# Merged depthwise kernels: stored with eight channels innermost, turned by TensorE, their zeros stored later

## The chip, the cores and the metric

One core of a Trainium2 chip runs the whole program. The metric is the time of one execution on the device in microseconds, the median over runs. Engine names: PE (TensorE: matmuls, with PEld its weight loads), DVE (VectorE), ACT (ScalarE), POOL (GpSimd), SP (SyncE, which here only issues DMAs). ACT, POOL and SP issue DMAs, each on a queue of its own; all queues share 16 DMA engines.

## The reference

Four layers on x of [8, 384, 32, 32], float32. Layer 0 is an RMS norm, a Mamba block run forwards and backwards over the 1024 pixels, and a gated 3x3 depthwise convolution. Layer 1 is a 1x1 / 3x3 / 1x1 convolution, linear attention and an MLP. The change touches what prepares layers 2 and 3, which are depthwise convolutions with large kernels:

```
# layer 2: seven depthwise convolutions (13x13, 5x5, 7x7, 7x7 dilated 2, 3x3 dilated 3, 4, 5), each
# with a batch norm, added up
out = bn_eval(dwconv(x, w_lk, 1), bn_gamma[0], ...)
for i, (w, r) in enumerate(zip(branch_ws, dilates)):
    out = out + bn_eval(dwconv(x, w, r), bn_gamma[i + 1], ...)
# layer 3: 1x1 product with a batch norm and a shortcut, then 13x13 depthwise + a scale per channel, GELU
x_pw = bn(einsum('bchw,oc->bohw', x, pw_w), ...) + x
out = bn(dwconv(x_pw, dwk_w), ...) + bn(x_pw * dw1_w, ...)
return gelu(out)
```

All kernels of a layer and their norms fold into one 13x13 kernel per channel (layer 2: `g2`, layer 3: `g3`) and one bias.

## The kernel before

**Stages.** A prologue (the first part of layer 0 for image 0, constants, and the merged kernels g2 and g3) leads into eight scans, one per image. Beside the scan of one image run the front of the next and layer 1 of the one before. After the last scan come the rest of layer 1 for the last image, convolution a (layer 2), the 1x1 product of layer 3 (`product`, `finish`) and convolution b (layer 3's 13x13).

**The prologue's chain.** `front(0)` loads x (`xi`), squares it on ACT, sums on PE (`ms_s`, `ms_b`), scales on DVE (`xn`), multiplies on PE (`in`), copies on ACT to `uz` and stores that to DRAM (`u_d`). From there it is loaded shifted (`ut`), convolved on PE (`c`), and passed through Silu on ACT (`uc`, L805). `dl_d` and `v_d` are then stored through POOL's queue and loaded by SP for the scan. In the scan, each unit is exponentials on ACT (`da`), products and scans on DVE (`du` L958, `hs` L970), a multiplication on POOL (L979) and sums on PE (`acc`).

**The merged kernels.** `kernels` (L171) runs interleaved with `front(0)`. For each third of the channels it loads the weights through SP, clears a tile of [128 channels, 4 shifts, 63 rows, 4 columns] on POOL (L205, L221), and merges the kernels into rows 25 to 37 of it with small DVE instructions (`merge`, L190, L192). The other rows stay zero: they are the border that makes a Toeplitz matrix of the row index. Six POOL DMAs of 504 KB (L216, L230) store the whole tiles, zeros included, to `g2_d` and `g3_d` in DRAM, channel outermost. The tiles are taken from the eight buffers `hs` that the scan uses later.

**The windows.** Convolutions a and b work on 48 blocks of eight channels. A block's weights are one tile `tp` of [128, 8, 128]: for each of four column shifts e, 32 partitions, one for each image row, hold the rows of the Toeplitz matrix. Each shift is one DMA of 128 KB (`load_windows`, L250). In DRAM, partition p starts 16 bytes after partition p-1, and each of the eight channels is a run of 512 bytes. There are 20 such tiles. For convolution a the first 20 blocks are loaded by POOL, from the moment when the scan's memory is free; the others, and those of convolution b, by SP and ACT in turn. In `conv` (L371) a group of four channels is four times four matmuls, which run side by side on four column groups of PE; their weights are the slice

```
tp[:, c, :].rearrange("p (j t) -> p j t", t=KT)[:, :, t]
```

that is, 32 elements at a step of 16 bytes. The images are loaded as `xt_a` (POOL, with a short SP load of the last image from `x2i_d`) and `xt_b` (POOL, from `xp_d`), and DVE copies them shifted. Results of a go through `yt` to `y2_d`, those of b through GELU on ACT (`ot`) to `out`, in pieces of 128 bytes.

**The order of the work.** The functions give only dependencies. The order on every engine is written by a planner (`Plan`): it places all instructions by rank (the longest way to the end, plus a number from the table `BIAS` for each family such as ('Pool', 'tp_a<g2_d')) with its own estimate of each one's duration. So a change in one place can move instructions anywhere. A DMA that is issued also waits for an earlier one whose completion counter it takes over; there are eight counters for POOL's DMAs and eight for those of SP and ACT.

Of the kernel before, what the change touches and what calls it, by code (L numbers as in the profile page):

```python
# [11 lines left out]
FP = mybir.dt.float32  # L12
# [61 lines left out]
def tile_layers(  # L74
# [44 lines left out]
    g2_d = dram.tile([C, NSH, TG, KT], FP, tag="g2_d", name="g2_d")  # L119
    g3_d = dram.tile([C, NSH, TG, KT], FP, tag="g3_d", name="g3_d")  # L120
# [50 lines left out]
    def kernels(small, large):  # L171
# [3 lines left out]
        off = H - 1 - KS // 2  # L175

        def merge(g, src, k, d, scale, first):
            lo = KS // 2 - d * (k // 2)

            step = NSH // gcd(NSH, d)  # L180
            for a in range(min(step, k)):
                n = len(range(a, k, step))
                kx = lo + d * a
                dst = g[
                    :, kx % NSH, off + lo : off + lo + d * (k - 1) + 1 : d,
                    kx // NSH : kx // NSH + (n - 1) * (d * step // NSH) + 1 : d * step // NSH,
                ].rearrange("p b a -> p a b")
                sv = src[:, a::step, :]
                if first:
                    nc.vector.tensor_scalar_mul(dst, sv, scale)  # L190
                else:
                    nc.vector.scalar_tensor_tensor(dst, sv, scale, dst, ALU.mult, ALU.add)  # L192

        def column(t, n, name):
            return t[:, :n].rearrange("p (q i t) -> p q i t", q=NSH, i=TG)
# [3 lines left out]
        gn = NSH * TG * KT  # L199
        for c in range(NC):  # L200
# [15 lines left out]
            nc.gpsimd.dma_start(g2_d[c * P : (c + 1) * P].rearrange("p q i t -> p (q i t)"), t[:, :gn])  # L216
# [9 lines left out]
            mid = g[:, m % NSH, off + m, m // NSH : m // NSH + 1]  # L226
# [3 lines left out]
            nc.gpsimd.dma_start(g3_d[c * P : (c + 1) * P].rearrange("p q i t -> p (q i t)"), t[:, :gn])  # L230
# [4 lines left out]
        yield 1  # L235

    wins = {}

    def load_windows(g_d, tag, n, queues, behind=None):
# [3 lines left out]
        tp = wins["pool"].tile([P, NCH, TP], FP, tag="tp", name=f"tp_{tag}_{n}", bufs=N_WIN)  # L243
        for e in range(NSH):
            at = H * ((n % 2 * 2 + e) % NSH)
            win = bass.AP(
                g_d.tensor, g_d[NCH * n, e, 0, 0].offset,
                [[KT, H], [NSH * TG * KT, NCH], [1, TP]],
            )
            made = queues[e % len(queues)].dma_start(tp[at : at + H], win)  # L250
# [5 lines left out]
    def windows(queues):  # L256
        for n in range(N_WIN):
# [5 lines left out]
              cw1_t, cw2_t, qkv_t, proj_t, w1, w2, headmask, mask8, mask8_t, kernels, windows)  # L263
# [5 lines left out]
    with tc.tile_pool(name="cx", bufs=2, reuse_waits="tile") as cxp, tc.tile_pool(  # L269
# [15 lines left out]
        def conv(g_d, src_d, last_d, tag, put, far):  # L285
# [67 lines left out]
            for g in range(NQ):  # L353
# [7 lines left out]
                for t in range(KT):  # L361
                    for e in range(4):
# [4 lines left out]
                        else:  # L367
# [5 lines left out]
                            tp[:, c, :].rearrange("p (j t) -> p j t", t=KT)[:, :, t], rhs,  # L373
# [116 lines left out]
def _layers01(tc, nc, B, xv, x2_d, x2i_d, dram, ident, mean_w, eps5, eps6, one, half, minus1, vec, bns, bnt,  # L490
              rs, rsm, inproj_t, xproj_t, dtproj_t, outproj_t, taps1, taps3, taps3b, sel, alog,
              cw1_t, cw2_t, qkv_t, proj_t, w1, w2, headmask, mask8, mask8_t, kernels, windows):
# [10 lines left out]
    with ExitStack() as ctx:  # L503
# [499 lines left out]
        def fold():  # L1003
# [37 lines left out]

        prepare = kernels(
            lambda name: scanp.tile([P, L], FP, tag="hs", name=name, bufs=N_HS),
            lambda name: scanp.tile([P, L], FP, tag="hs", name=name, bufs=N_HS),
        )
# [310 lines left out]
        jobs = [[first, 36, 0, rounds // 4, 0], [fold(), 36, 0, rounds, 0]]  # L1356
# [63 lines left out]
class Step:  # L1420
    def __init__(self, ins, kind_of):
# [28 lines left out]
        else:  # L1450
# [3 lines left out]
            if self.engine == "Pool":  # L1454
                self.ns = 80 + n * (2.21 if self.kind == "InstTensorTensor" else 2.55)
# [395 lines left out]
def draft(nc, tc, bias):  # L1851
# [15 lines left out]
BIAS = {('Activation', 'acc<y0'): -13900,  # L1867
 ('Activation', 'bc_d<xd'): -60800,
 ('Activation', 'center<center'): -86000,
 ('Activation', 'da<dlt'): 1600,  # L1870
 ('Activation', 'dl<dt'): -21300,
 ('Activation', 'dw<dw'): -18000,
 ('Activation', 'fold<fold'): -148900,
 ('Activation', 'gbias<biasq_d'): -35300,
 ('Activation', 'h_d<hh'): 31500,
 ('Activation', 'hh<h'): 600,
 ('Activation', 'hm<mf'): -501200,
 ('Activation', 'kp<phi_k'): -30300,
 ('Activation', 'kv<kvs'): -61000,
 ('Activation', 'kvp<kvp'): 315700,  # L1880
 ('Activation', 'kvp_d<kvp'): -900,
 ('Activation', 'lc<lc'): -7500,
 ('Activation', 'ms_r<ms_r'): -70000,
 ('Activation', 'ms_r<ms_s'): -2100,
 ('Activation', 'ot<cv_b'): -58600,
 ('Activation', 'out<ot'): 4700,
 ('Activation', 'phi_k<kv_kp'): 53000,
 ('Activation', 'phi_q<q'): -391200,
 ('Activation', 'qp<phi_q'): -2200,
 ('Activation', 'rz<den'): -3500,  # L1890
 ('Activation', 'rz<rz'): -7300,
 ('Activation', 'sq<xi'): -91600,
 ('Activation', 'tm<pw'): 145400,
 ('Activation', 'tp_b<g3_d'): -31500,
 ('Activation', 'u_d<uz'): -31400,
 ('Activation', 'uc<c1'): -11000,
 ('Activation', 'ud_d<ud'): -33900,
 ('Activation', 'uz<in'): 500,
 ('Activation', 'var_r<var_r'): 110900,
 ('Activation', 'var_r<var_s'): -14600,  # L1900
 ('Activation', 'vs<xx'): -111800,
 ('Activation', 'vt<kv_vt'): 2000,
 ('Activation', 'vt<ones'): 20900,
 ('Activation', 'x2_d<turn'): 53700,
 ('Activation', 'xd<xd'): 6900,
 ('Activation', 'xt_b<xp_d'): -50500,
 ('Activation', 'yf_d<yt'): 10800,
 ('Activation', 'yt<cv_a'): -38000,
 ('Activation', 'z_d<uz'): 140600,
 ('DVE', 'bias1<fold'): -72900,  # L1910
 ('DVE', 'bias2<bias2'): 191000,
 ('DVE', 'bias2<bn_t'): 26600,
 ('DVE', 'bias3<bn_t'): -43000,
 ('DVE', 'biasc<fold'): -4000,
 ('DVE', 'biasf<fold'): -122000,
 ('DVE', 'carry<hs'): 67300,
 ('DVE', 'dlt<pk'): 40000,
 ('DVE', 'du<vr'): -602900,
 ('DVE', 'dwh<pk'): -99500,
 ('DVE', 'g2<kw'): 15500,  # L1920
 ('DVE', 'g3<g3'): 28000,
 ('DVE', 'g3<k3'): 143300,
 ('DVE', 'hs<da'): 151900,
 ('DVE', 'kv<kvs'): 2000,
 ('DVE', 'lc<lc'): -96000,
 ('DVE', 'ln<xx'): -42300,
 ('DVE', 'qp<qp'): 59300,
 ('DVE', 'uc<dl'): -44000,
 ('DVE', 'ud<uc'): -36600,
 ('DVE', 'v2<pk'): -51500,  # L1930
 ('DVE', 'var_r<var_r'): -111500,
 ('DVE', 'var_r<var_s'): -214500,
 ('DVE', 'xn<xi'): 56200,
 ('DVE', 'xo0<tm'): 7000,
 ('DVE', 'xo1<tm'): 32500,
 ('DVE', 'xo2<tm'): -19000,
 ('DVE', 'xr<lc'): -35800,
 ('DVE', 'xt_a<xt_a'): 4200,
 ('DVE', 'xt_b<xt_b'): 3000,
 ('DVE', 'xx<c2'): 2300,  # L1940
 ('DVE', 'xx<op'): 46000,
 ('DVE', 'xx<pj'): 62500,
 ('DVE', 'zr<acc'): 16300,
 ('PE', 'acc<hs'): 1600,
 ('PE', 'acc<y0'): -4600,
 ('PE', 'c1<ut'): -35800,
 ('PE', 'c2<dw'): 21200,
 ('PE', 'center<fold'): 44100,
 ('PE', 'cv_a<xt_a'): -7500,
 ('PE', 'cv_b<xt_b'): -146300,  # L1950
 ('PE', 'den<qp'): 111100,
 ('PE', 'dt<xd'): -98100,
 ('PE', 'fold<bn_t'): 200,
 ('PE', 'fold<v2'): 13800,
 ('PE', 'h<xx'): 18800,
 ('PE', 'kss<spread'): -102400,
 ('PE', 'kvp<pj'): -65300,
 ('PE', 'kvs<zero'): -16000,
 ('PE', 'lc<lc_i0'): -81500,
 ('PE', 'mf<ln'): -4300,  # L1960
 ('PE', 'mo<hm'): 3100,
 ('PE', 'ms_b<ms_r'): -26700,
 ('PE', 'ms_s<sq'): -45000,
 ('PE', 'op<g'): 14200,
 ('PE', 'op<zr'): 20200,
 ('PE', 'pb<bias2'): 2500,
 ('PE', 'pj<qp'): 800,
 ('PE', 'pw<yp'): -12000,
 ('PE', 'q<xx'): 5300,
 ('PE', 'rzb<rz'): -12000,  # L1970
 ('PE', 'var_b<var_r'): -5500,
 ('PE', 'var_s<vs'): -37200,
 ('PE', 'var_s<xx'): -37300,
 ('PE', 'xd<uc'): -111000,
 ('Pool', 'dl_d<dl'): 19000,
 ('Pool', 'fold<fold'): 89500,
 ('Pool', 'g2<'): -4200,
 ('Pool', 'g2_d<g2'): -43500,
 ('Pool', 'g3<'): -5700,
 ('Pool', 'g3_d<g3'): -20000,  # L1980
 ('Pool', 'g_d<zr'): -18700,
 ('Pool', 'h_d<zero'): -78000,
 ('Pool', 'hs<hs'): -7300,
 ('Pool', 'spread<'): -10800,
 ('Pool', 'tp_a<g2_d'): -39000,
 ('Pool', 'turn<'): 51500,
 ('Pool', 'u_d<zero'): 17400,
 ('Pool', 'v_d<uc'): 229400,
 ('Pool', 'w1_d<fold'): 80300,
 ('Pool', 'x1_d<xr'): -300,  # L1990
 ('Pool', 'x2i_d<xx'): 148700,
 ('Pool', 'xn_d<xn'): -36200,
 ('Pool', 'xn_d<zero'): -18000,
 ('Pool', 'xp_d<xo0'): -23200,
 ('Pool', 'xp_d<xo1'): 60200,
 ('Pool', 'xp_d<xo2'): -48000,
 ('Pool', 'xt_a<'): -200,
 ('Pool', 'xt_b<xp_d'): 51700,
 ('Pool', 'y2_d<yt'): -36000,
 ('SP', 'bct<bc_d'): -7000,  # L2000
 ('SP', 'c1<c1_d'): -2000,
 ('SP', 'c2<c2_d'): -2000,
 ('SP', 'dlt<dl_d'): 19600,
 ('SP', 'dw_i0<h_d'): 2000,
 ('SP', 'dw_i1<h_d'): -23200,
 ('SP', 'dw_i2<h_d'): -10600,
 ('SP', 'dw_i3<h_d'): -202400,
 ('SP', 'g<g_d'): -5000,
 ('SP', 'k3<in_dwk'): 55000,
 ('SP', 'kvw<kvp_d'): -17800,  # L2010
 ('SP', 'kw<in_l2k'): 18200,
 ('SP', 'lc_i0<xn_d'): 610500,
 ('SP', 'lc_i1<xn_d'): 2000,
 ('SP', 'lc_i2<xn_d'): 12200,
 ('SP', 'lc_i3<xn_d'): 4000,
 ('SP', 'pj<in_proj_t'): -36600,
 ('SP', 't3<in_taps3'): 8000,
 ('SP', 't3b<in_taps3b'): 80000,
 ('SP', 'tp_a<g2_d'): 14500,
 ('SP', 'tp_b<g3_d'): 165900,  # L2020
 ('SP', 'turn<x2i_d'): 213400,
 ('SP', 'ut<u_d'): -183800,
 ('SP', 'w1<w1_d'): 125000,
 ('SP', 'w2<in_w2'): 4700,
 ('SP', 'win<in_inproj_t'): -42500,
# [124 lines left out]
```

## Time and profile before

| | |
|---|---|
| median of 3 runs | 4487.36 us (4484.69 to 4489.67) |
| the profiled execution | 4489.67 us, of which the profile's span is 4487.8 |
| PE, DVE, ACT, POOL busy | 3960.7, 3643.9, 2618.5, 2615.8 us |
| DMA | 748530 packets, 976 MB, 217 GB/s over the span |
| loads of windows (`tp_a`, `tp_b`) | 384 of 128 KB: 80 by POOL, 152 by SP, 152 by ACT |
| median time to landing | tp_a 8.1 (POOL), 7.3 (SP), 6.3 (ACT); tp_b 6.8 (SP), 6.1 (ACT) |
| stores of merged kernels | 6 of 504 KB, 9.5 us to landing |
| weight loads of convolutions a and b | 3072 each, 137 ns median |

Busy times overlap: what counts is which engine is full in which stage, and which wait ends last there. A line of the stages names begin and end in us, length, busy time of each engine with the number of instructions, the clock granted to PE, the share of time in which the 16 DMA engines were busy, and GB/s. A line of the chain names start, length and what the path to the end went through. A line of a DMA queue names packets, MB, and the time that its packets took as a share of 16 engines over the window; q0 is POOL's, q1 SP's and q10 ACT's queue. One MB is counted as a million bytes there, and KB of a load as 1024.

### The profile page before, as it was taken

The page shows a single profiled execution, that of the slowest core. Times are in us where ns is not written, and L with a number is a line of the kernel's source. Part 1 is how long each engine was busy: PE and PEld are TensorE (multiplying, and loading weights), DVE is VectorE, ACT ScalarE, POOL GpSimd, SP SyncE. Part 2 cuts the span into 40 slices and gives each one's busy share as a digit, 9 for nine tenths or more (in the row PEclk, how much of TensorE's full clock was granted, in tenths as well). Part 3 has the DMA queues.
Part 4 walks back from the last instruction along what each step waited for, and adds up shares of the span by engine and source line. Part 5 has one row for each costly group of instructions (what it writes and reads, how often), then busy time and mean ns, then how long its engine had stood idle before and what let it go on. Part 6 is the DMA issues. An engine that isn't in the chain of part 4 may idle for free.

```text
span 4487.8 us, 95449 instructions
## 1 busy us (share of the span) xinstructions
PE 3960.7 (88%) x38454; PEld 1600.2 (36%) x38454; DVE 3643.9 (81%) x3843; ACT 2618.5 (58%) x3701; POOL 2615.8 (58%) x1567
## 2 busy tenths in 40 slices
PE   5687798999988999999999899989889979989978
PEld 1121233233323332343333323332243433376456
DVE  2999989999999889999999899989999801176365
ACT  3666657865786578667866886578566503101212
POOL 2686757676667657775777576757675830043111
PEclk8687899999999999999999999999999969999989
DMA  9587786588658866896788668856845661398998
GB/s 263 187 256 254 244 233 232 201 256 252 225 197 252 251 224 206 258 269 207 239 248 256 208 225 252 261 200 229 232 136 171 194 151 51 88 242 220 270 200 160
DMA packets 748530, 976.06 MB, mean 217 GB/s; under 512 B 256840, under 2 KB 433464, under 8 KB 746552
## 3 DMA queue, kind: packets, MB, share of 16 engines
q1 hardware_dynamic: 504864, 680.88, 51.4%
q0 software_dynamic: 47616, 170.88, 11.7%
q10 hardware_dynamic: 195608, 118.21, 9.9%
q8 instruction: 303, 4.96, 0.5%
q14 instruction: 139, 1.14, 0.1%
HBM read 737.32 MB, written 232.40 MB: 216 GB/s over the span
## 4 chain that ended last, share of the span: by engine, by line
PE 49%; DVE 18%; DMA 15%; issue 7%; ACT 6%; POOL 2%; SPq 1%; ACTq 1%; DVEq 0%; POOLq 0%
DVE hs L970 11%; PE mo L623 8%; PE mf L623 7%; DVE du L958 4%; DMA dw_i<-h_d 3%; PE cv_a L371 3%; PE acc L643 3%; PE pj L623 3%; PE cv_b L371 2%; ACT da L953 2%; PE in L623 2%; PE q L623 2%; PE op L623 2%; PE kv_vt L623 2%; PE c L623 2%
## 5 line engine op out<-in xcount | busy, mean ns | idle before, releaser
L979 POOL TENSOR_TENSOR hs<-hs,bct 128x1024 f32<-128x1024 f32 x768 | 2174.3, 2831 | 884.4 <-DVE carry L975 498.9
L953 ACT ACTIVATE da<-dlt,neg_a 128x512 f32<-128x512 f32 x1536 | 1021.4, 714 | 577.8 <-DVE hs L970 461.0
L958 DVE TENSOR_TENSOR du<-vr,bct 128x1024 f32<-128x1024 f32 x768 | 979.9, 1276 | 54.3 <-DMA vr<-v_d 28.6
L970 DVE TENSOR_TENSOR_SCAN hs<-da,carry,du 128x512 f32<-128x512 f32 x768 | 946.4, 1267 | 39.4 <-PE acc L648 4.3
L970 DVE TENSOR_TENSOR_SCAN hs<-da,du 128x512 f32<-128x512 f32 x768 | 900.0, 1208 | 35.5 <-ACT da L953 9.0
L648 PE MATMUL acc<-hs,selt 128*32 128x512 f32 x2304 | 543.4, 634 | 78.9 <-POOL hs L979 78.6
L623 PE MATMUL mf<-ln,w 128*32 128x512 f32 x4608 | 579.1, 614 | 36.6 <-ACT uc L805 20.4
L623 PE MATMUL mo<-hm,w 128*32 128x512 f32 x4608 | 564.1, 595 | 0.3 <-DVE xx L1286 0.3
L643 PE MATMUL acc<-hs,selt 128*32 128x512 f32 x768 | 413.3, 627 | 22.6 <-POOL hs L979 22.5
L623 PE MATMUL in<-xn,win 128*32 128x512 f32 x2304 | 307.6, 629 | 24.7 <-DMA win<-in_inproj_t 15.4
L623 PEld LDWEIGHTS mf<-ln,w 128*32 128x32 f32 x4608 | 167.1, 113 | 383.9 <-issue 299.2
L953 ACT ACT_TABLE_LOAD x224 | 287.4, 1283 | 21.4 <-DMA dlt<-dl_d 7.5
L623 PEld LDWEIGHTS mo<-hm,w 128*32 128x32 f32 x4608 | 166.9, 110 | 325.3 <-issue 293.9
L648 PE MATMUL dw<-dw_i,t3b 96*32 96x512 f32 x1056 | 222.0, 686 | 16.2 <-DMA dw_i<-h_d 16.1
L371 PE MATMUL cv_b<-xt_b,tp_b 128*32 128x256 f32 x3072 | 192.6, 410 | 47.3 <-ACT ot L480 37.9
L313 POOL DMA_DIRECT2D xt_a<-x_d x48 | 40.1, 835 | 303.8 <-PE var_b L623 121.4
L344 DVE COPY xt_b<-xt_b 32x2496 f32<-32x2496 f32 x94 | 136.4, 1452 | 88.0 <-DMA xt_b<-xp_d 78.9
L371 PE MATMUL cv_a<-xt_a,tp_a 128*32 128x256 f32 x3072 | 179.1, 391 | 27.1 <-DVE xt_a L338 10.9
L648 PEld LDWEIGHTS acc<-hs,selt 128*32 128x32 f32 x2304 | 121.7, 114 | 173.7 <-POOL hs L979 144.2
L371 PEld LDWEIGHTS cv_b<-xt_b,tp_b 128*32 128x32 f32 x3072 | 147.3, 143 | 92.9 <-ACT ot L480 45.3
L371 PEld LDWEIGHTS cv_a<-xt_a,tp_a 128*32 128x32 f32 x3072 | 156.6, 139 | 50.0 <-issue 27.7
L623 PEld LDWEIGHTS in<-xn,win 128*32 128x32 f32 x2304 | 99.8, 115 | 196.4 <-issue 156.4
(211 smaller groups left out, 5637.9 us busy)
## 6 DMA issues: line engine op xcount, KB each, us to landing
dlt<-dl_d SPq DMA_DIRECT2D x384, 256.0 KB, 4.5
vr<-v_d SPq DMA_DIRECT2D x384, 256.0 KB, 5.0
bct<-bc_d SPq DMA_DIRECT2D x256, 256.0 KB, 5.3
ut<-u_d SPq DMA_DIRECT2D x192, 257.5 KB, 5.4
lc_i<-xn_d SPq DMA_DIRECT2D x192, 228.8 KB, 6.5
dw_i<-h_d SPq DMA_DIRECT2D x192, 228.8 KB, 6.2
w<-w_d SPq DMA_DIRECT2D x64, 576.0 KB, 6.6
w<-in_w SPq DMA_DIRECT2D x64, 576.0 KB, 5.3
```

Source lines behind the costliest of these rows:

```text
L313: nc.gpsimd.dma_start(own[:, 0:near], src_d[n].rearrange("h b c w -> h (b c w)"))
L344: nc.vector.tensor_copy(xt[at[e] : at[e] + e * H, :, 0 : RL - e - (e - 1)], xt[at[0] : at[0] + e * H, :, e : RL - (e - 1)],)
L371: nc.tensor.matmul(ps[H * e : H * (e + 1), 0:BW], tp[:, c, :].rearrange("p (j t) -> p j t", t=KT)[:, :, t], rhs, start=(t == 0), stop=(t = ...
L623: product = nc.tensor.matmul(ps[lo:hi], lhs[:, lo:hi], rhs, start=start, stop=stop, skip_group_check=True)
L643: first = product()
L648: tc.keep_in_program_order(product())
L953: nc.scalar.activation(da[:, bass.ts(j, HALF)], dlt[:, bass.ts(j, HALF)], AF.Exp, scale=neg_a[:, g, r : r + 1],)
L958: nc.vector.tensor_mul(pairs(du), pairs(vt), bct[r][:, 0:1, :].to_broadcast([P, 2, HALF]),)
L970: nc.vector.tensor_tensor_scan(t[:, s][:, way], da[:, s][:, way], du[:, s][:, way], k_c if second else 0.0, ALU.mult, ALU.add,)
L979: made.append(nc.gpsimd.tensor_mul(pairs(t), pairs(t), bct[r][:, 1:2, :].to_broadcast([P, 2, HALF])))
```

## The change

The merged kernels get another layout in DRAM: [48 blocks, 4 shifts, 63 rows, 4 columns, 8 channels], channels innermost. A row of a block is then 128 bytes, and the window of one partition is one run of 4 KB that starts 128 bytes after that of the partition before. The tile `tp` has the same order, so a matmul's 32 weights lie 128 bytes apart.

The tile in which DVE merges has 32 rows for each shift instead of 63, of which 13 are used. `turn` brings the channels innermost: 16 matmuls with the identity for each of the six tiles, and one ACT copy from PSUM to a tile `s2`, which permutes. `store` writes the 13 rows with kernel values, by four POOL DMAs for each tile (26.6 KB each, in pieces of 128 bytes). The zero rows are written from the tile `zero` by `borders`, eight POOL DMAs of 307 KB in pieces of 800 bytes, as a job within the first scan. The planner counts 100 ns more for a copy on POOL, and the table `BIAS` is replaced.

```diff
-    g2_d = dram.tile([C, NSH, TG, KT], FP, tag="g2_d", name="g2_d")
+    g2_d = dram.tile([NB_C, NSH, TG, KT, NCH], FP, tag="g2_d", name="g2_d")
...
-            return t[:, :n].rearrange("p (q i t) -> p q i t", q=NSH, i=TG)
+            return t[:, :n].rearrange("p (q i t) -> p q i t", q=NSH, i=H)
+
+        def store(g_d, g, c):
+
+            n = P // NCH
+            made = turn(g, f"{g_d.tensor.name}_{c}")
+            for q in range(NSH):
+                nc.gpsimd.dma_start(
+                    g_d[n * c : n * (c + 1), q, low : low + KS].rearrange("n i t c -> i n (t c)"),
+                    made[H * q : H * q + KS].rearrange("p (n w) -> p n w", n=n),
+                )
...
-        gn = NSH * TG * KT
+        gn = NSH * H * KT
...
-            nc.gpsimd.dma_start(g2_d[c * P : (c + 1) * P].rearrange("p q i t -> p (q i t)"), t[:, :gn])
+            store(g2_d, g, c)
...
+    def borders(zero, held):
+
+        info = mybir.DependencyInfo(mybir.DependencyClass.NoSync, mybir.DependencyReason.DATA)
+        low = H - 1 - KS // 2
+        half = NB_C * NSH // 2
+        part = low * KT * NCH // 4
+        src = zero[:half, 0:part]
+        src = bass.AP(src.tensor, src.offset, [src.ap[0], [0, 4], [1, part]])
+        for g_d in (g2_d, g3_d):
+            flat = g_d.rearrange("n e i t c -> (n e) (i t c)")
+            for p in range(2):
+                for at in (0, low + KS):
+                    dst = flat[p * half : (p + 1) * half, at * KT * NCH : (at + low) * KT * NCH]
+                    made = nc.gpsimd.dma_start(dst.rearrange("p (a b) -> p a b", a=4), src)
+                    tc.add_manual_dep(made.ins, held[0].ins.name, info, reason="later")
+                    yield 1
...
-        tp = wins["pool"].tile([P, NCH, TP], FP, tag="tp", name=f"tp_{tag}_{n}", bufs=N_WIN)
+        tp = wins["pool"].tile([P, H, KT, NCH], FP, tag="tp", name=f"tp_{tag}_{n}", bufs=N_WIN)
...
-                g_d.tensor, g_d[NCH * n, e, 0, 0].offset,
-                [[KT, H], [NSH * TG * KT, NCH], [1, TP]],
+                g_d.tensor, g_d[n, e, 0, 0, 0].offset,
+                [[NCH * KT, H], [1, NCH * TP]],
...
-                            tp[:, c, :].rearrange("p (j t) -> p j t", t=KT)[:, :, t], rhs,
+                            tp[:, :, t, c], rhs,
...
+        def turn(g, name):
+
+            ps = long_psum(f"kt_{name}")
+            t = s2(f"kt_{name}")
+            for a in range(KT):
+                for q in range(NSH):
+                    nc.tensor.matmul(
+                        ps[H * q : H * (q + 1), a * P : (a + 1) * P], g[:, q, :, a], ident,
+                        start=True, stop=True, skip_group_check=True,
+                    )
+            nc.scalar.copy(
+                t.rearrange("p (n t c) -> p t n c", t=KT, c=NCH), ps.rearrange("p (t n c) -> p t n c", t=KT, c=NCH)
+            )
+            return t
...
-        jobs = [[first, 36, 0, rounds // 4, 0], [fold(), 36, 0, rounds, 0]]
+        jobs = [[first, 36, 0, rounds // 4, 0], [fold(), 36, 0, rounds, 0], [borders(zero, held), 8, 0, rounds, 0]]
...
-                self.ns = 80 + n * (2.21 if self.kind == "InstTensorTensor" else 2.55)
+                self.ns = (180 if self.kind == "InstTensorCopy" else 80) + n * (2.21 if self.kind == "InstTensorTensor" else 2.55)
...
-BIAS = {('Activation', 'acc<y0'): -13900,
- ('Activation', 'bc_d<xd'): -60800,
...
+BIAS = {('Activation', 'acc<y0'): 2000,
+ ('Activation', 'bc_d<xd'): -37800,
...
```

## The prediction

> **What bounds the kernel now.** I read four views: the page, busy time by stage, the chain that ended last, and the DMA queues inside single stages. From the page, span and where DMA is full:
>
> ```profile
> span 4487.8 us, 95449 instructions
> PE 3960.7 (88%) x38454; PEld 1600.2 (36%) x38454; DVE 3643.9 (81%) x3843; ACT 2618.5 (58%) x3701; POOL 2615.8 (58%) x1567
> DVE  2999989999999889999999899989999801176365
> DMA  9587786588658866896788668856845661398998
> ```
>
> DVE fills the scans (about 100 to 3584 us); after them it is idle and DMA fills up. The stages, with PE, PEld, DVE, ACT, POOL busy time, PE clock, DMA share and GB/s:
>
> ```profile
> 100.00:3584.00 3484.00, 3124.80 (x29009) 1119.85 (x29012) 3258.51 (x3327) 2420.77 (x3359) 2397.13 (x1209) 0.94 0.73 228
> 3584.00:3668.00 84.00, 53.62 (x188) 10.73 (x184) 0.00 (x0) 4.63 (x9) 39.60 (x68) 0.59 0.98 211
> 3668.00:3904.00 236.00, 227.59 (x2442) 92.29 (x2434) 23.15 (x36) 58.72 (x97) 2.82 (x12) 0.97 0.20 61
> 3904.00:4103.00 199.00, 172.97 (x2972) 151.68 (x2975) 160.00 (x142) 17.17 (x46) 97.48 (x158) 0.96 0.90 210
> 4103.00:4250.00 147.00, 135.32 (x412) 62.53 (x404) 40.09 (x104) 37.84 (x50) 13.78 (x20) 0.97 0.98 270
> 4250.00:4488.00 238.00, 192.63 (x3072) 147.34 (x3072) 134.59 (x95) 45.06 (x96) 34.31 (x44) 0.90 0.97 180
> ```
>
> So: scans bound by DVE (94% busy), then 84 us bound by DMA (0.98), 236 us by PE, convolution a mostly by PE, the 1x1 product (147 us) by DMA, convolution b by DMA. The chain says it by piece (start, length, what):
>
> ```profile
> 37.99 10.39 DMA u_d<-uz
> 49.13 13.30 DMA ut<-u_d
> ...
> 3636.02 23.77 DMA dw_i<-h_d
> ...
> 4264.44 13.85 DMA tp_b<-g_d
> ...
> 4414.79 68.81 PE cv_b L371 x1148
> ```
>
> The last piece gives PE's own pace: 1148 matmuls, in fours, are 287 x 0.240 us. 768 fours need 184 us; convolution b took 233 (4250.7 to 4483.6), convolution a 195. That is 49 and 11 us of stalls.
>
> The windows (tp) are what the change alters. Queues in 4270 to 4400, then the SP queue in 80 to 105 us (packets, MB, share of 16 engines). In the first, SP (q1) loads windows alone, POOL (q0) xt_b alone:
>
> ```profile
> q0 software_dynamic: 1923, 7.70, 25.9%
> q1 hardware_dynamic: 13220, 6.37, 24.8%
> ```
>
> ```profile
> q1 hardware_dynamic: 2678, 4.90, 56.5%
> ```
>
> In engine time per MB (share x length x 16 / MB): windows in 512-byte pieces 24.8% x 130 x 16 / 6.37 = 81 us; xt_b, in packets of 4 KB to the same 32 partitions, 70; ut and bct, 2-KB rows to 128 partitions, 46. The same sum gives windows 82 in convolution a (ACT queue 3920 to 4090: 22.2%, 7.34 MB), 79 on POOL at 3600 to 3660, 70 in the product stage (ACT queue 4130 to 4230: 16.1%, 3.70 MB).
>
> **The change part by part.**
>
> *Windows, 4-KB runs instead of eight of 512 bytes; bytes and number of loads the same.* No row shows a 4-KB window load. It lies between 81 (no gain) and 46 us per MB (best row). I take 70, that of xt_b: same engines, same 32 partitions, long packets. Convolution b loads 112 x 0.131 = 14.7 MB: (81-70) x 14.7 / 16 = 10 us off its DMA-bound part (4250 to 4415). Bounds 0 and 32. Convolution a: the same bytes, (82-70) x 14.7 / 16 = 11, but only 11 us there are not PE's own, and the chain puts some on the short xt_a loads from x2i_d, so 7; bounds 0 and 11. In 3584 to 3668 PE waits for dw_i while POOL pushes 75 windows through the same engines: 9.8 MB x (79-70) / 16 = 5.5 us; bounds 0 and 20. Product stage: already 70, so 0; bounds 0 and 10.5 MB x 24 / 16 = 15. What is late next: in b, the out stores (128-byte packets) and PE's 184 us.
> The Trainium skill's page "DMA: Bandwidth & Descriptors" (Specifications) puts full rate at 512 bytes and up, which speaks against the change; the rows here differ by 81 to 70. By the rule the windows would gain nothing, and the sum below would be about 0.
>
> *Weights at a step of 128 bytes instead of 16.* tp[:, :, t, c] steps over 32 elements. Loads of 32 weights:
>
> ```profile
> L371 PEld LDWEIGHTS cv_b<-xt_b,tp_b x3072: 134/137/178, 4250.6 to 4483.0; 128*32 128x32 f32 x192
> ```
>
> The contiguous acc<-hs,selt has median 110 ns: the step of 16 bytes goes with 27 ns. Loads overlap: 147 us for 768 fours, 192 ns per four under a pace of 240. I take 0: all 32 elements lie apart already. One more such 27 ns makes 192 x 164/137 = 230, still under 240. Bounds 0 and, with three times 27 (218 ns, 306 per four), 66 ns x 1536 fours = +100 us.
> The page "SBUF — State Buffer" (Door 1: The DMA port swizzle) gives 16-byte lines, a penalty for each access that crosses to a new one; both steps touch 32 lines, so by it the sum stays as it is. No row here has 128 bytes.
>
> *Turning in the prologue.* 96 matmuls on PE, 6 copies on ACT. Twelve of the 24 fours stand ahead of the last `in` product, on the chain to u_d. 32 ms_b matmuls took 1.93 us, so 12 x 0.24 = 2.9 us. The copies (0.59 us each, row uz<-in) run beside PE. The last three ACT copies wait for stores of the first three kernels (three s2 buffers); behind them is the first Silu, which waited 21.6 us for PE anyway. That cover hides them; without it they cost 1.8 us plus the landing of a store (4 to 11 us).
>
> *Stores.* Before: six of 504 KB on POOL, 23 to 41 us; in 35 to 50 POOL's queue used 46.7% for 2.23 MB, 50 us per MB, so 3.1 MB took 9.7 us of all engines. They stand beside the chain's 10.4 and 13.3 us, which elsewhere land in 5.1 and 5.4. After: 24 stores, 4992 pieces of 128 bytes. The out stores of 4410 to 4488 (50462 packets, 58.5%) give 14.5 ns each: 4.5 us. Net -5, plus 2.9 of PE: -2. Bounds: -10 (both landings normal, PE paid) and +8: 24 issues of 0.6 to 0.8 us on POOL ahead of xn_d, biasq_d and then dl_d, each waiting for an earlier one to land; and on DVE the third xn of the second half now stands behind the g2 merges of the third channel group, whose weights landed at 35.5 us.
>
> *Zeros.* Eight POOL stores of 307 KB among the first multiplies and the dl_d and v_d stores of the second half. POOL: 8 x 0.76 us (row xn_d<-zero), and it idles 1.4 us in each 3.7 there; DMA: 2.5 MB x 50 / 16 = 8 us in 110 to 140, where the share is 0.79 to 1.03. Behind them wait dl_d and v_d, needed units later. I take +1; bounds 0 and +8. The memsets of g shrink (0.95 to about 0.53 us each, off the chain): 0.
>
> *The order.* The table of biases is new, so all five queues are reordered. The scans have the same DVE work, 3258 us; only their 226 us of DVE idle can move. Table switches in ACT's order fall from 365 to 357, 8 x 1.28 us on an engine with slack. No row gives a sign: 0, bounds -20 and +20 (a tenth of the idle).
>
> **Sum:** -10 -7 -5.5 -2 +1 = -23.5. The profiled execution took 4489.67 (span 4487.8, 1.9 around it), 2.3 above the median of three, 4487.36. So 4466.2 for it, 4464 at the median.
>
> **Rivals.**
> A. *The port of 32 partitions is the limit, not the piece.* For it: POOL already packs windows into packets of 2.7 KB (911 packets, 2.49 MB at 3600 to 3620) and pays 79. Against: 82 falls to 70 where loads to 128 partitions run beside. Only prologue, zeros and order remain: about 4487.
> B. *Weight loads slow down.* The place is L371; it decides from 137 x 240/192 = 171 ns. Against: nothing overlaps less so far. At 218 ns +100, of which convolution b hides some 40 in its DMA stalls: 4464 + 60 = 4524, slower.
> C. *Long runs reach 46 us per MB.* -32 -11 -20 -15 -2 +1 = -79: about 4408.
> D. *The new order loses in the scans*, a tenth of DVE's idle: 4464 + 22 = 4486.
>
> **How the numbers follow.** Forecast 0.50, own range 4445 to 4478; C or part of it 0.17; A 0.15; D 0.10; B 0.08. One measurement here tells 0.2%, 9 us, from nothing: below 4478 is faster, above 4496 slower. Forecast and C are faster (0.67); of A and D, 0.15 within and 0.10 slower with the prologue's upper bound; B slower. I reach down past half of C, 4420, and up past A and D with their bounds, 4503; B is left out.
>
> **What would show it.** Right: windows at about 70 us per MB in 4270 to 4400, convolution b near 223 us, cv_b weight loads at 137 ns, dw_i done some 5 us earlier, first scan at or before 105.9 us. Wrong: windows still at 80 (A), weight loads over 171 ns (B), DVE idle in the scans moved by more than 20 us (D, or an unforeseen gain).

## The result, and the profile after

The changed kernel takes 4458.24 us (median of 4 runs, 4452.17 to 4461.4) against 4486.34 (median of 4, 4484.69 to 4489.67): 0.9935 of the time, 95% interval 0.9918 to 0.9952. The forecast was 4464. The total came close, but partly by luck: two of its main terms (convolution b and the order of the scans) and a smaller one (the prologue) were wrong, with opposite signs. The rest of this document is about them.

The page of the changed kernel, span, busy time and DMA share:

```profile
span 4456.7 us, 95889 instructions
PE 3926.6 (88%) x38646; PEld 1561.6 (35%) x38646; DVE 3626.5 (81%) x3843; ACT 2619.9 (59%) x3707; POOL 2616.8 (59%) x1593
DVE  2999999999999899999999999999989801186365
DMA  8678686589768866886688668866844671297898
```

Busy time by stage, with boundaries at the starts of the first and last scan instruction on DVE, of the first matmul on c2 (the second 1x1 convolution of layer 1, here for the last image) and of the first and last matmuls of the two convolutions (columns: stretch, its length, PE, PEld, DVE, ACT, POOL, PE clock, DMA share, GB/s):

```profile
110.10:3553.00 3442.90, 3078.22 (x28890) 1074.48 (x28890) 3238.09 (x3321) 2417.85 (x3357) 2378.16 (x1201) 0.93 0.73 230
3553.00:3644.90 91.90, 65.27 (x294) 13.20 (x298) 4.20 (x6) 4.99 (x8) 42.41 (x84) 0.66 0.98 234
3644.90:3891.70 246.80, 231.23 (x2454) 83.08 (x2448) 25.91 (x39) 58.68 (x97) 4.78 (x10) 0.96 0.19 60
3891.70:4079.40 187.70, 175.97 (x3071) 160.74 (x3072) 156.90 (x142) 17.54 (x47) 102.43 (x160) 0.99 0.85 224
4079.40:4221.30 141.90, 129.06 (x310) 57.45 (x307) 39.49 (x102) 37.69 (x49) 13.19 (x19) 0.96 0.89 274
4221.30:4452.50 231.20, 186.97 (x3072) 151.19 (x3072) 134.35 (x95) 44.33 (x95) 36.65 (x44) 0.89 0.94 184
```

The kernel before, cut at the same events, for the two stages in which the forecast failed:

```profile
105.90:3571.30 3465.40, 3109.36 (x28906) 1116.26 (x28910) 3253.09 (x3322) 2417.48 (x3355) 2386.59 (x1193) 0.93 0.73 228
4250.70:4483.20 232.50, 192.24 (x3072) 147.28 (x3072) 133.93 (x94) 44.59 (x95) 34.31 (x44) 0.90 0.98 182
```

Cut this way for both, the span moved by 31.1 us:

| stretch | before | after | difference | forecast |
|---|---|---|---|---|
| start to first scan instruction | 105.9 | 110.1 | +4.2 | -2 |
| first to last scan instruction | 3465.4 | 3442.9 | -22.5 | +1 (zeros), 0 (order) |
| last scan instruction to first c2 matmul (the dw_i loads) | 95.5 | 91.9 | -3.6 | -5.5 |
| c2 to convolution a | 247.0 | 246.8 | -0.2 | 0 |
| convolution a | 195.0 | 187.7 | -7.3 | -7 |
| 1x1 product | 141.9 | 141.9 | 0 | 0 |
| convolution b | 232.5 | 231.2 | -1.3 | -10 |
| tail | 4.6 | 4.2 | -0.4 | 0 |

Convolution b kept its length although the windows did get cheaper there. The queues of the changed kernel in 4240 to 4370 (packets, MB, share of 16 engines):

```profile
q10 hardware_dynamic: 46026, 11.89, 49.7%
q0 software_dynamic: 1919, 7.67, 27.2%
q1 hardware_dynamic: 2301, 6.29, 20.9%
```

SP's queue (q1) loads windows alone: 20.9% x 130 x 16 / 6.29 = 69 us of engine time per MB, 81 before. The same sum gives 62 in convolution a (ACT's queue in 3900 to 4070: 16.4%, 7.16 MB; 82 before), 67 on POOL (3575 to 3635: 52.7%, 7.58 MB; 79 before) and 44 in the 1x1 product (ACT's queue in 4100 to 4200: 11.5%, 4.16 MB; 70 before). The weights at the step of 128 bytes cost almost nothing, 141 ns for 137 (min, median, max):

```profile
L398 PEld LDWEIGHTS cv_b<-xt_b,tp_b x3072: 131/141/223, 4221.3 to 4452.3; 128*32 128x32 f32 x192
```

So in convolution b about 11 us of DMA work went away and PE did not notice. What PE waited for there, in the changed kernel (total, times, longest):

```profile
PE cv_b L398 <- ACT ot L507: 38.4, 6, 11.9
PE cv_b L398 <- DVE xt_b L371: 5.9, 1, 5.9
PE cv_b L398 <- issue: 2.5, 1, 2.5
```

And in the kernel before:

```profile
PE cv_b L371 <- ACT ot L480: 37.9, 11, 6.8
PE cv_b L371 <- issue: 9.3, 2, 7.0
```

PE waits for Gelu copies (`ot`) that free a PSUM buffer, not for windows. ACT is busy 44 of 231 us, so it isn't short of time; it stands still. What ACT itself waited for there before a Gelu, transfers alone (changed kernel):

```profile
ACT ot L507 <- DMA out<-ot: 63.0, 6, 16.8
ACT ot L507 <- DMA tp_b<-g_d: 30.4, 3, 17.0
```

A piece of the chain of the changed kernel (start, length, what):

```profile
4253.90 5.26 DMA tp_b<-g_d
4259.19 0.31 ACTq L277
4259.56 5.36 DMA tp_b<-g_d
4264.99 8.04 DMA tp_b<-g_d
4273.10 5.66 DMA tp_b<-g_d
4278.76 0.46 ACT ot L507
```

ACT's program is one row: Gelu, out issue, window issue. In it an issue waits for one of eight completion semaphores that all transfers of SP and ACT share (the planner's `LANES = 8`), that is for an earlier transfer to land. Here the chain goes through four window loads in a row, 25 us. In the last 17.0 of them ACT ran no Gelu: the longest wait of the list above.

The chain of the kernel before has such pieces too (ACTq is an issue on ACT):

```profile
4300.02 9.02 DMA out<-ot
4309.11 0.40 ACTq L481
4309.56 0.48 ACT ot L480
```

### The profile page after: what moved, and what is told of

It reads as the page before. It is cut to its first block, busy times and chain, and to the rows that moved or that the text cites. A ratio compares the mean times of both kernels' runs of the same rounds, so it can differ in the third digit from the quotient of the medians.

```text
span 4456.7 us, 95889 instructions
## 1 busy us (share of the span) xinstructions
PE 3926.6 (88%) x38646; PEld 1561.6 (35%) x38646; DVE 3626.5 (81%) x3843; ACT 2619.9 (59%) x3707; POOL 2616.8 (59%) x1593
## 4 chain that ended last, share of the span: by engine, by line
PE 57%; DVE 15%; DMA 13%; ACT 7%; issue 4%; POOL 1%; SPq 1%; ACTq 1%; DVEq 0%; POOLq 0%
PE mo L650 9%; DVE hs L997 9%; PE mf L650 8%; DVE du L985 3%; PE acc L670 3%; PE cv_a L398 3%; PE pj L650 3%; PE in L650 3%; PE cv_b L398 3%; ACT da L980 3%; PE pw L454 3%; PE op L650 2%; PE kv_vt L650 2%; DMA dw_i<-h_d 2%; PE dw L675 2%
## 5 line engine op out<-in xcount | busy, mean ns | idle before, releaser
L985 DVE TENSOR_TENSOR du<-vr,bct 128x1024 f32<-128x1024 f32 x768 | 967.7, 1260 | 51.5 <-DMA vr<-v_d 27.6
L650 PE MATMUL mf<-ln,w 128*32 128x512 f32 x4608 | 568.1, 604 | 31.0 <-ACT uc L832 18.7
L398 PE MATMUL cv_b<-xt_b,tp_b 128*32 128x256 f32 x3072 | 187.3, 404 | 46.7 <-ACT ot L507 38.4
L675 PE MATMUL dw<-dw_i,t3b 96*32 96x512 f32 x1056 | 202.5, 670 | 10.7 <-DMA dw_i<-h_d 10.4
L675 PEld LDWEIGHTS acc<-hs,selt 128*32 128x32 f32 x2304 | 117.0, 114 | 158.2 <-POOL hs L1006 131.8
L670 PEld LDWEIGHTS acc<-hs,selt 128*32 128x32 f32 x768 | 83.3, 114 | 236.2 <-issue 152.5
```

The costliest lines, as they stand in the source:

```text
L398: nc.tensor.matmul(ps[H * e : H * (e + 1), 0:BW], tp[:, :, t, c], rhs, start=(t == 0), stop=(t == KT - 1), skip_group_check=True,)
L650: product = nc.tensor.matmul(ps[lo:hi], lhs[:, lo:hi], rhs, start=start, stop=stop, skip_group_check=True)
L670: first = product()
L675: tc.keep_in_program_order(product())
L985: nc.vector.tensor_mul(pairs(du), pairs(vt), bct[r][:, 0:1, :].to_broadcast([P, 2, HALF]),)
```

## Experiments on convolution b: whose bound it was

An edit in convolution b leaves the planned order as it was up to the 1x1 product (in the traces DVE's and POOL's instructions follow one another as before), so these runs differ from there on alone. In the cuts of code below, comments after `#` are not in the kernels.

**Windows on SP.** ACT no longer issues windows in convolution b:

```diff
-                        load_windows(g_d, tag, m, [nc.sync, nc.scalar])
+                        load_windows(g_d, tag, m, [nc.sync, nc.scalar] if last_d is not None else [nc.sync])
```

> The changed kernel, but in convolution b all window loads that the convolution itself issues go out on SP (before: two of the four of a block on SP, two on ACT); nothing else moves until the end of the 1x1 product. Theory Q (ACT's queue): convolution b hardly gained because PE waits for the Gelu copies, and those stand on ACT behind window and out issues that each wait for an earlier transfer to land; then convolution b falls from 231.6 us to 205-220 and PE's wait for ACT ot from 38 us to under 25. Rival E (engines): the 16 DMA engines with the 128-byte out stores set the pace, and what the windows saved was eaten by the rest; then 229-234 us, and the wait for ot stays above 33.

Measured: 4405.96 us, 0.9811 of before (0.9796 to 0.9826). Convolution b took 184.2 us, below the range that theory Q gave. Its stage and PE's waits in it:

```profile
4214.00:4398.20 184.20, 177.87 (x3072) 155.82 (x3072) 133.13 (x94) 44.76 (x95) 45.93 (x44) 0.99 1.08 232
```

```profile
PE cv_b L398 <- DVE xt_b L371: 4.0, 1, 4.0
PE cv_b L398 <- DMA xt_b<-xp_d: 2.6, 1, 2.6
PE cv_b L398 <- ACT ot L507: 2.1, 4, 1.1
```

The wait for Gelu fell from 38.4 to 2.1 us, and the stage to PE's own 184 us (768 fours at the pace that the prediction read from the last stretch). The same bytes went through the same 16 engines, at 232 GB/s instead of 184. E falls: the engines were not what set the pace. The DMA share went up to 1.08, so a share near 1 was no ceiling. ACT's waits changed in length more than in total:

```profile
ACT ot L507 <- DMA tp_b<-g_d: 62.3, 31, 3.9
ACT ot L507 <- DMA out<-ot: 8.8, 2, 6.6
```

That is 71.1 us in 33 waits, none over 6.6, against 93.4 us in 9 waits of up to 17.0. Many short ones don't reach PE here; a few long ones did.

**Out stores on SP, or on POOL.** The other way to empty ACT's row, with the windows still half on ACT:

```diff
-            nc.scalar.dma_start(
+            nc.sync.dma_start(        # second kernel: nc.gpsimd
                 ov[g * P : (g + 1) * P], ot.rearrange("p (b w) -> p b w", w=W)
```

> The changed kernel, but the 96 out stores of convolution b go out on SP instead of ACT; the windows stay half on ACT. Q: ACT's Gelu copies no longer stand behind the out issues, convolution b falls to 205-222 us. E: bytes, pieces and engines are the same, 229-234 us. If out stores held up the windows on SP instead, it would be longer than 234.

> The changed kernel, but the 96 out stores go out on POOL, which is busy 37 of 235 us there. Q: both the waits of the out issues and their share of the two hardware queues are gone from ACT and SP: 195-215 us for convolution b, total 4425-4445. E: 229-234 us. A third possibility: xt_b loads, which are on POOL too, come late behind stores that wait for their Gelu; then PE waits for DVE xt_b by more than 10 us.

Measured: 4425.14 us (0.9849, 0.9831 to 0.9867) with convolution b at 198.9, and 4422.87 (0.9851, 0.9831 to 0.9871) with 193.5. Both are shorter than 229, so Q again (below even its ranges, as in the first run), and both are longer than the first run. On SP the windows now stand behind stores that wait for their Gelu; PE waits 7.0 us for windows and 10.2 for DVE xt_b. On POOL the wait for DVE xt_b is 7.4 us (5.9 in the changed kernel), under the 10 that the third possibility asked for, and the last store ends 11.0 us after the start of the last matmul instead of 4.2.

**The kernel before with its windows on SP.** The same one-line edit:

> The kernel before, with the same edit as in the first of these runs: all windows of convolution b on SP, in 512-byte pieces. It gives the worth of the long pieces once ACT is out of the way: if Q is right and the saving of 81 to 69 us per MB was only hidden, this convolution b is 8-15 us longer than that of the first run (217-233 us). If the piece does not matter for the stage at all, the two are within 3 us.

Measured: 4449.52 us, 0.9916 (0.9893 to 0.994). Its convolution b, in 512-byte pieces:

```profile
4244.10:4439.30 195.20, 180.79 (x3072) 150.96 (x3072) 130.33 (x90) 44.69 (x95) 41.74 (x44) 0.99 1.12 217
```

195.2 against 184.2: the long pieces are worth 11.0 us once ACT is out of the way, within the 8 to 15 that were expected, though the stage itself lies below its 217 to 233. That is the term of the forecast (10), which the changed kernel had earned and could not collect. With 512-byte pieces PE still waits 10.5 us for Gelu there (16 times, at most 1.7) and 0.9 for windows; so the saving seems to reach PE through ACT's issues, which is read from one list of waits and not tested. Later pairs say the same: with windows on SP convolution b took 195.2 and 191.3 us in the two kernels with 512-byte pieces, and 184.2, 180.4, 182.2, 183.2 and 185.6 in the five with 4 KB.

## Experiments on the scans: layout or order

The scans gave 22.5 us that no term of the forecast had. The old and new layout and the old and new table make four kernels; both missing ones were run with the windows on SP, so that convolution b doesn't blur the total. The planner's new price of a POOL copy is in both of them. Of each table the cut shows the first line.

```diff
-BIAS = {('Activation', 'acc<y0'): 2000,      # new layout, planned with the table of before
+BIAS = {('Activation', 'acc<y0'): -13900,
...
-BIAS = {('Activation', 'acc<y0'): -13900,    # old layout, planned with the new table
+BIAS = {('Activation', 'acc<y0'): 2000,
```

> The first run's kernel (changed layout, windows of convolution b on SP), planned with the old table of biases. Judged by the scans (first to last scan instruction on DVE: 3465.4 us before, 3442.9 after). Theory O (the new order brought the 22 us): with the old numbers the scans go back to 3450-3480. Rival L (the layout or its stores brought them, whatever the order): 3436-3448. Convolution b stays at 184-187 us in both.

> The kernel before with windows of convolution b on SP, planned with the new table (and its price of 180 ns for a POOL copy): the old layout under new numbers. O: the scans fall to 3436-3450. L: they stay at 3452-3468 (before and its twin with windows on SP: 3465 and 3455). Convolution b 192-198 us in both.

Measured: 4424.65 us (0.986, 0.9838 to 0.9881) and 4429.97 (0.9883, 0.9853 to 0.9912). The scans in us, one value for each profiled execution:

| | old table | new table |
|---|---|---|
| old layout | 3465.4, 3454.9 | 3425.4 |
| new layout | 3467.9 | 3442.9, 3440.3, 3446.1, 3441.8, 3450.7 |

The column decides, not the row: O. The five values in one cell come from one and the same order up to the last image, and the two in another likewise, so a profiled execution repeats to some 10 us here. From the mean of the one cell to that of the other the whole change is worth 16 us in the scans (3460.2 to 3444.4), where the pair of traces above showed 22.5. The table alone is worth 23.5 with the new layout (3467.9 to 3444.4) and 34.8 with the old one (3460.2 to 3425.4, below the range that was given), each with a single trace on one side. Part of the 34.8 is only moved: in that kernel the stretch after the scans takes 103.5 us, against 95.5 and 95.3 in the other two with the old layout.

The whole times of the four kernels, as shares of the time of the kernel before, are 0.9916 (old layout, old table), 0.9860 (new layout, old table), 0.9883 (old layout, new table) and 0.9811 (both new). So of some 4487 us, with the windows of convolution b on SP, the layout is worth 25 or 32 and the table 15 or 22; for the 15 alone the two intervals overlap.

**One number nudged.**

```diff
- ('SP', 't3<in_taps3'): -185200,
+ ('SP', 't3<in_taps3'): 40000,
```

> The first run's kernel with one number of the new table changed (the SP load of the taps3 weights, -185200 to +40000). The order is the same up to the seventh scan unit and differs after it. It gives how far an order moves the scans by itself: if O is right and the gain is a matter of chance collisions between DVE and POOL, the scans move by 5-25 us from the 3440 of the first run; if they stay within 4 us, the gain belongs to something that all these orders share.

Measured: 4404.13 us, 0.9812 (0.9784 to 0.984), scans 3442.5. By the expectation's own words (within 4 us) that speaks for something all these orders share; but one order repeats only to 10 us, so 2 us can't settle it. On the way the two orders differed more than at the end: at the 865th of the 1536 scan instructions the nudged kernel stood 15 us behind the first run, counted from the first scan instruction of each. So the gain doesn't hang on a single order; two orders from nearly one table have it. Which of its numbers carry it was not tried.

Where the time is inside the scans can be read. DVE's busy time fell from 3253.1 to 3238.1 us although it does the same work, and its idle time from 212.3 to 204.8. The busy part is in the products with two inputs in SBUF: `du` and `ud` became shorter, `uc` longer. Groups of the kernel before (busy us, mean ns | idle before):

```profile
L958 DVE TENSOR_TENSOR du<-vr,bct 128x1024 f32<-128x1024 f32 x768 | 979.9, 1276 | 54.3 <-DMA vr<-v_d 28.6
L841 DVE TENSOR_TENSOR uc<-dl,uc 128x512 f32<-128x512 f32 x96 | 67.7, 740 | 16.3 <-ACT dl L833 12.9
L838 DVE TENSOR_TENSOR ud<-uc,uc 128x512 f32<-128x512 f32 x48 | 66.6, 1388 | 27.7 <-ACT uc L805 27.2 <-PE var_s L1233 0.4
```

And of the changed kernel:

```profile
L985 DVE TENSOR_TENSOR du<-vr,bct 128x1024 f32<-128x1024 f32 x768 | 967.7, 1260 | 51.5 <-DMA vr<-v_d 27.6
L868 DVE TENSOR_TENSOR uc<-dl,uc 128x512 f32<-128x512 f32 x96 | 84.2, 913 | 19.1 <-ACT dl L860 16.0 <-DVE ud L865 0.5
L865 DVE TENSOR_TENSOR ud<-uc,uc 128x512 f32<-128x512 f32 x48 | 45.2, 944 | 38.7 <-ACT uc L832 36.0 <-PE dt L856 1.4 <-PE var_s L1276 1.0
```

`ud` has a median of 684 ns but a mean of 1388 before. Two lines of the timeline of the kernel before show why, DVE first:

```profile
482.36 2.84 DVE L838 TENSOR_TENSOR ud<-uc,uc 128x512 f32<-128x512 f32 x1
```

```profile
482.21 2.44 POOL L979 TENSOR_TENSOR hs<-hs,bct 128x1024 f32<-128x1024 f32 x1
```

POOL began 0.15 us earlier and ended at 484.65; the DVE product ended at 485.20, 0.55 us later. It stood until POOL was done. Take the DVE instructions `du`, `ud`, `uc` and `carry` of each trace that lasted more than 1.3 times what is usual for their kind (1232, 678, 680 and 156 ns): before there are 53, of which 51 overlap a POOL product, with 69.1 us beyond the usual in all; in the changed kernel 37, of which 34 overlap one, with 54.4 us. Overlap by itself proves little: 635 of the other 738 `du` before overlap a POOL product as well. The ends tell more: all 50 of the `du`, `ud` and `uc` among the 53, and all 30 among the 37, end 0.54 to 0.56 us (512 elements) or 1.09 to 1.10 us (1024) after a POOL product does, so they stood until it was done. The new table lets them meet less often: in all runs with it 36 to 46 are stretched, in the three with the old one 52 to 54.

That is not the whole gain. The nudged kernel's scans are as short as those of the first run with DVE busy for 3247.9 us and idle for 194.6 (3235.8 and 204.5 in the first run), and in the kernel with the old layout and the new table idle time fell most (185.4). What shortens the idle time was not found. The Trainium skill, in "SBUF — State Buffer" (Who interferes with whom), calls the port pair that DVE and GpSimd share an exclusive lock: a two-input DVE instruction contends with a GpSimd instruction that reads SBUF, and the loser blocks fully. The traces agree for `ud`, `uc` and `du`. The scan instruction has two inputs in SBUF too, but it never rose above 1.284 us (medians 1.210 and 1.270 for its two forms), though 1376 of the 1536 before overlap a POOL product: for it the measurement decides against the rule.

## Experiments on the windows ahead of convolution a, and on the prologue

**Windows after the last dw copy.** In the stretch from the last scan instruction to c2, PE waits for dw_i while POOL loads 10.5 MB of windows. Of the queues of the changed kernel there (3553 to 3644.9):

```profile
q0 software_dynamic: 3840, 10.49, 47.9%
q1 hardware_dynamic: 7696, 9.10, 42.5%
```

The edit, on top of the first run's kernel, makes these loads wait in earnest for the copy of the last dw product; behind it lie 245 us in which PE is the bound and the DMA share was 0.19:

```diff
-                nc.scalar.copy(dws[h][:, c, :], ps)
+                marks.append(nc.scalar.copy(dws[h][:, c, :], ps))
...
-        ahead = windows([nc.gpsimd])
+        ahead = None
         for _ in seconds[B - 1]:
             tick()
-            next(ahead, None)
+            if ahead is None and len(marks) == 6 * B:
+                ahead = windows([nc.gpsimd], marks[-1])    # each load waits for marks[-1]
+            if ahead is not None:
+                next(ahead, None)
```

> The first run's kernel, but the 80 window loads that POOL issues ahead of convolution a wait for the last dw copy, so that they run beside the 245 us that PE bounds instead of beside the dw_i loads. Theory W (window bytes hold up dw_i: 10.5 of 21.5 MB there): from the last scan instruction to the first c2 matmul 50-72 us instead of 93.8, total 4365-4390. Rival H (the landing of h_d and dw_i alone sets it): 85-94 us, total 4400-4412. If the late windows come in the way of later loads, convolution a or the 245 us get longer instead.

Measured: 4376.83 us, 0.9752 (0.9732 to 0.9771). The stretch and the one after it:

```profile
3562.70:3618.90 56.20, 44.63 (x294) 11.76 (x298) 4.22 (x6) 4.99 (x8) 3.43 (x4) 0.88 0.73 195
3618.90:3863.60 244.70, 230.04 (x2452) 85.12 (x2444) 25.88 (x39) 58.69 (x97) 43.50 (x90) 0.96 0.37 104
```

W: 56.2 us (93.0 in the first run), and the windows fit under the next stretch, which kept its length. The landing of a dw_i load fell from 14.1 to 5.3 us:

```profile
dw_i<-h_d SPq DMA_DIRECT2D x24, 228.8 KB, 5.3
```

The forecast had seen these windows only as something that gets some 11% cheaper, for 5.5 us; their place was worth 37. The whole kernel gained less than that against the first run (4405.96 to 4376.83), as its profiled scans and prologue came out 10 and 4 us longer with the same order.

**The taps load on POOL.** In the prologue of the changed kernel the chain shows an issue on SP that takes 9 us, between the fourth and the fifth ut load; before, that load stood ahead of them:

```profile
54.08 9.17 SPq L631
63.35 8.03 DMA ut<-u_d
```

```diff
-            nc.sync.dma_start(t[:96], ap)
+            (nc.gpsimd if name == "t3_0" else nc.sync).dma_start(t[:96], ap)
```

> The kernel of the run before (windows of convolution b on SP, those of convolution a after the last dw copy), with the first image's taps3 load issued by POOL instead of SP, where its issue stands for 9.2 us between the fourth and the fifth ut load. Theory T (that load is what makes the changed prologue longer): the first scan instruction at 104-108 us instead of 108.4-112.1 (five kernels with this prologue), total 4368-4380. Rival P (the turn on PE and the late landing of u_d make it, the taps load only fills a wait): it stays at 108-113. In both the scans may move by up to 10 us either way, because the order after it changes.

Measured: 4375.54 us, 0.9725 (0.9712 to 0.9738, an interval that overlaps that of the run before), inside the expected total, but with the first scan instruction at 122.7, not 104 to 108, and scans of 3432.3. T is not confirmed, nor is P as it was put. From the landing of u_d to the first product of c passed 16.1 us instead of 20.3, so the load did cost some 4 us there. But the x load on the chain landed 4.4 us later than in the changed kernel, and the planner now put all eight zero stores ahead of POOL's first product. Part of POOL's timeline, and the last step of the chain:

```profile
102.79 0.71 POOL L260 DMA_DIRECT2D g_d<-zero  x1 [0.56 <-DMA v_d<-uc]
105.03 2.83 POOL L260 DMA_DIRECT2D g_d<-zero  x4 [1.53 <-issue]
```

```profile
109.87 11.38 DMA vr<-v_d
```

With the zeros in flight a load of v took 11.4 us to land (median of all such loads before: 5.0), and the first scan waited for it. No run without the zeros there was made, so that they are what slowed this load is likely and not shown. In the changed kernel, where they come among the first products, the first 96 scan instructions took 198.5 us against 205.0 before, so there they cost nothing that can be seen.

## Why the prediction was right or wrong

- **Windows, rate (right).** 70 us per MB was taken; 69, 62 and 67 came in convolution b, convolution a and on POOL. Rival A (the port of 32 partitions) falls. In the 1x1 product the rate went to 44, near C's end, with no gain in time, as the forecast's 0 had it.
- **Windows in convolution b, -10 (wrong in the kernel, right in itself).** The step that failed is "off its DMA-bound part (4250 to 4415)". A DMA share of 0.97 and a chain full of DMA pieces were read as engines that set the pace. They did not: with the windows moved to another issuing engine the kernel before itself fell from 232.5 to 195.2 us with the same bytes. The chain had the answer in it (ACTq and ACT ot between the DMA pieces), and so had the list of PE's waits, which the prediction does not use. Behind that wait the term measures 11.0.
- **Convolution a, -7 (right).** -7.3 in the pair. Over all profiles 512-byte pieces took 195.0, 197.7 and 197.3 us, 4-KB pieces 186.9 to 189.3.
- **dw_i, -5.5 (right mechanism, size hidden by the order).** -3.6 in the pair, and -4.4 on the means of two traces before (95.5 and 95.3) and four of the change with these windows in place (91.9, 93.0, 89.3 and 89.8). But the new table moved this stretch too: the last store of h_d is issued 24.1 us after the last scan instruction, before 17.2. The new layout under the old table, with that store again at 17.2, took 86.3 us: the long pieces are worth 9.1 there, in one trace, and the order gave about 5 back.
- **Weight loads, 0 (right).** 141 ns for 137, far under the 171 from which rival B decides, and in the run with windows on SP PE keeps its 184 us.
- **Prologue, -2 (wrong sign, cause not settled).** +4.2 in the pair. Two profiles with the prologue of before gave 105.9 and 109.1, five with the changed one 108.4 to 112.0: about +3 on the means, beside a spread of 3 to 4. The crossed kernels say no more: 113.7 with the new layout under the old table, 111.2 with the old layout, and so without the turn, under the new one. The 1.75 us of turning that lie on the chain, which the forecast had at 2.9, and the taps load among the ut loads are in the trace; no run tells them apart.
- **Zeros, +1 (right within what can be seen).** They cost nothing visible where the change puts them; where the last run put them, the first scan waited for a load that took 11.4 us.
- **Order, 0 with bounds of 20 (wrong).** The step that failed is "only their 226 us of DVE idle can move". Busy time moved too, by 15.0 us, because a DVE product that meets a POOL product takes up to 2.8 us longer; idle time moved by 7.5. (The fall of table switches on ACT from 365 to 357, which the forecast names there, is in neither trace: both have 565 table loads.) And a table of numbers was taken for chance of either sign, where the runs show that the new one is shorter with both layouts.

The total held by luck: 22.5 us in the scans that had not been foreseen stood in for 8.7 that convolution b withheld and for 6.2 of prologue, and the profiled execution fell by 31.1 us for a forecast of 23.5. With ACT out of the way the layout by itself is worth 25 to 32, which the sum of its terms comes near.

## What to carry to other kernels

A stage with a DMA share near 1 need not be bound by DMA, as convolution b shows: read who the bound engine waits for, and if that is an engine with little busy time, look at what stands in its program between two pieces of its work. Loads that can wait on an earlier transfer did best here on an engine that computes nothing. And when a transfer gets cheaper, ask first whether it could move: here a place beside 245 us of PE work was worth 37 us, the cheaper piece 4 to 9.

## What the runs showed of the hardware

- The size of a piece told beyond 512 bytes: the same windows to the same 32 partitions cost 76 us of engine time per MB in 512-byte pieces and 58 in 4-KB pieces in the two runs with all windows of convolution b on SP (36.6% for 10.00 MB, and 31.1% for 11.13 MB, of 130 us x 16 engines). The Trainium skill's page "DMA: Bandwidth & Descriptors" (Specifications) gives 512 bytes as the least size for the full rate; the measurement decides, and it differs.
- One order of instructions, executed again, gave scans from 3440.3 to 3450.7 us and a first scan instruction from 108.4 to 112.0. A difference between two traces of under 10 us in the scans, or of under 4 in the prologue, is not a result by itself in this kernel.
